# A two-layer graph kernel: its opening reordered, a stream of block products started six instructions earlier, and rows returned in five parts

## The chip, the cores and the metric

The kernel runs on one core of a Trainium2 chip. The metric is the device time of one execution in microseconds (us). A core has five engines with queues of their own: TensorE (PE) for matmuls and transposes, VectorE (DVE), ScalarE (ACT) and GpSimd (POOL) for everything elementwise, and SyncE (SP), which here only issues transfers (DMAs). ACT's queue can issue transfers as well. Each engine runs its instructions in order.

## The reference

x has N = 2708 rows of D = 256; adj is 2708 x 2708, sparse in values but stored dense. Layer 0 makes two steps of a diffusion over adj and of an attention of x with itself that keeps, in each row, only the largest probabilities until their sum reaches 0.9:

```python
R = adj + eye;  R = R / R.sum(-1)
for n in range(2):
    A  = top_p_attention(Xa, W1, W2, W3)     # q = Xa W1' W2', k = Xa W3', softmax, keep the top 0.9, renormalise
    Xf = R @ Xf
    Xa = A @ Xa
    Z += Xf @ U1[n].T + Xa @ U2[n].T
x = layernorm(x + layernorm(x + Z))          # with ln_g, ln_b inside
# layer 1: graph attention, 4 heads of 64
Wh = x @ W;  e_ij = leaky_relu(s_i + s_j);  masked where adj is zero (the diagonal counts as one)
x = layernorm(x + softmax_j(e) @ Wh)
```

## The kernel before

**Tiles.** Rows are cut in 22 tiles: 16 of 128 rows and 6 of 110. Six `groups` hold four tiles each of one height (the last two). All heavy data is float32.

**The opening.** `query_weights` (L736) transposes w1 and multiplies it with w2, so that queries need one product. `turn_x` (L1420) transposes one group of x by TensorE into both halves of one two-bank tile `lg`; ACT copies the first half to `x_turned` (which lies in the buffer `ba`) and DVE the second. `project` (L749) makes keys and queries of a group: the products of both weights go to one bank, DVE copies the key's half (L765, to a buffer that the profile calls junk or kT) and ACT the query's (qT, L766); a DMA brings the copy for the other half of the partitions. A group that crosses a boundary of 512 columns is projected in two halves, both in the same bank.

**Terms and search.** `terms1` (L1253) multiplies a tile of x with U1 of both steps; ACT copies the result (L1263, L1264), and a DMA stores part of it (c1). Between the terms stand `slot`s: each advances generators that are under way. `search` makes a tile's logits (`scores`, L791, exponentials on ACT at L810) and finds the cut of the top 0.9: `candidates` by DVE's Max8 (L913), `settle` by a chain of small DVE instructions and two long passes over the row (L898 and L982, near 3 us each). `layer1_weights` (L1392) loads and prepares weights of layer 1.

**Attention steps.** `step(s, ...)` (L1345) goes over the 22 tiles; `weigh` (L274) multiplies the transposed probabilities of the tile, group by group, with the values. `turned` (L261) does a group's transposes into a bank `tr` (there is one) and an ACT copy to eT (L271); it runs one group ahead of its products. After each group, `between` runs, which calls `slot`. At the end of a tile ACT scales the result (xa, L1363); in step 0 a tile's queries and keys for step 1 follow (`after_attention0`: L774, L761).

**The block products.** R is never multiplied out plainly: POOL (`mixes`, L691) makes sums of quarters of adj, and `walks` (L1051) is a generator in which each `next(stream)` is one matmul of 128 columns (L1130), seven products of 11 matmuls for each pair of tiles in the manner of Winograd. The results are added up on DVE (L1140 y1, L1142 y2, L1148, L1150) and ACT. The operand `xm` and `xe` are re-blended between the two rounds: `reblend` (L1194), on DVE for T3 and T2 (L1024, L1026) in two parts each, the second of which needs the last rows of the first round. In step 1 every slot takes 11 or 12 instructions of the stream.

```python
if last:
    next(stream)              # in `between`, at the last tile of step 0
```

**Layer 1.** Scores of all pairs are formed on DVE (pt, L1644) with masks that come from adj: a DMA (L245, on SP), ACT's sign and square (L247, L248) and DVE's diagonal (L251). TensorE sums values (L1656) and denominators (L1666). It goes over two halves of the rows, g = 0 and 1. `beside(g, i)` (L1737) is called for each column tile i and puts other work between: at (0, 12) the rows kept in DRAM come back (xe<-xd, L1750, in two transfers), at i = 11 a row of sources is shared over the partitions (`share`, L217, and `spread`, L225). The last three tiles of layer 0 get x for their sums from `x_late`, loaded on SP at L1083 behind a POOL memset (L1076).

**Order.** PE, ACT, DVE and POOL run in the order that the program is written in (a manual schedule); SP's transfers are placed by a scheduler. A transfer waits, on its queue, for the landing of the transfer eight before it.

Of the kernel before, what the change touches and what calls it, by code (L numbers as in the profile page):

```python
# [1 line left out]

# [6 lines left out]
F32 = mybir.dt.float32  # L9
# [7 lines left out]
P = 128  # L17
# [3 lines left out]
CHUNK = 512  # L21
# [13 lines left out]


SPEND_BETWEEN, SPEND_1 = 14, (12, 11, 11, 12, 11, 11)
HELD, WAITING = 6, 4
SIDE = 32
LN2 = 0.6931471805599453  # L40
# [5 lines left out]
def kernel(  # L46
# [54 lines left out]

    HALF, PAIRS = D // 2, NT // 2
    xe = const.tile([P, NT, D + 2], F32, name="xe")
    for one in (HALF, D + 1):
        nc.gpsimd.memset(xe[:, :, one : one + 1], 1.0)

    wx = const.tile([P, DC, D + 2 * H], F32, name="wx")
    ident = const.tile([P, P], F32, name="ident")
    make_identity(nc, ident)
    minus_half = const.tile([P, 1], F32, name="minus_half")  # L110
    nc.gpsimd.memset(minus_half, -0.5)

# [7 lines left out]

    LATE = 3
    x_late = const.tile([P, LATE, D], F32, name="x_late")
    engines = {nc.tensor.engine, nc.scalar.engine, nc.vector.engine, nc.gpsimd.engine}

    def load_x(dst):
# [426 lines left out]
    def fast_layer0(ep, adjp):  # L552
# [28 lines left out]
        w1_sb = heldp.tile([P, D], F32, name="xa1")[:DA].rearrange("p (c d) -> p c d", c=DC)  # L581
        nc.scalar.dma_start(w1_raw, w1T.rearrange("(c p) e -> p c e", p=P))
        nc.scalar.dma_start(w2_sb, w2T)
        for h in range(2):
            nc.scalar.dma_start(wkqk[:, :, 2 * h, :], w3T.rearrange("(c p) e -> p c e", p=P))
        xm = keep.tile([P, NT, D], F32, name="xm")
        load_x(xm)
        for s in range(STEPS):
            for k, u in enumerate((u1T, u2T)):
                nc.sync.dma_start(u_sb[:, k, :, s], u[s].rearrange("(c p) e -> p c e", p=P))  # L590
        nc.sync.dma_start(g_sb, ln_g.partition_broadcast(P))
        nc.sync.dma_start(b_sb, ln_b.partition_broadcast(P))
# [143 lines left out]
        def query_weights():  # L736

            tr = free_bank()
            for c in range(DC):
                nc.tensor.transpose(tr[:DA, c, :], w1_raw[:, c, :], ident)  # L740
            nc.vector.tensor_copy(w1_sb, tr[:DA, 0:DC, :])
            for c in range(DC):
                tr = free_bank()
                nc.tensor.matmul(
                    tr[:, 0, :DA], w1_sb[:, c, :], w2_sb, start=True, stop=True
                )
                nc.vector.tensor_copy(wkqk[:, c, 1], tr[:, 0, :DA])

        def project(s, c0, w, pj, xT, copy_q, copy_k):  # L749

            for lo, hi, h in ((c0, min(c0 + w, HN), 0), (max(c0, HN), c0 + w, 1)):
                if lo >= hi:
                    continue
                here, there = slice(h * DA, (h + 1) * DA), slice((1 - h) * DA, (2 - h) * DA)
                at = slice(lo - c0, hi - c0)
                for c in range(DC):  # L760
                    nc.tensor.matmul(  # L761
                        pj[:, at], wkqk[:, c, h : h + 2].rearrange("p h e -> p (h e)"),
                        xT[:, c, at], start=(c == 0), stop=(c == DC - 1),
                    )
                copy_k(kT[s][here, lo - h * HN : hi - h * HN], pj[here, at])  # L765
                copy_q(qT[there, lo:hi], pj[there, at])  # L766
                nc.sync.dma_start(qT[here, lo:hi], qT[there, lo:hi])
# [283 lines left out]
        def walks():  # L1051
# [184 lines left out]
        def after_attention0(t, xa):  # L1236
# [8 lines left out]
            turn(xa, m, tp, nc.scalar.copy, xT)  # L1245
            yield
            if t % 2:
                pj = free_bank().rearrange("p a b -> p (a b)")
                project(1, off[t - 1], 2 * m, pj, both, nc.scalar.copy, nc.scalar.copy)
                yield  # L1250
            terms2(t, xT)

# [89 lines left out]
                if next(stream, True):  # L1342
                    break

        def step(s, cur, spend):  # L1345
            turned_first = None
            for t in range(NT):
                m = rows[t]
                e, rden = ready[t]
# [9 lines left out]
                def between(n):  # L1359
# [11 lines left out]
                    if (s, t) == (0, NT - 1):  # L1371
# [8 lines left out]
                def turn_next(n):  # L1380
                    u = t + n // len(groups)
                    if u == NT:
                        return None
                    return turned(ready[u][0], rows[u], n % len(groups), tpp, ps_tr, nc.scalar.copy)

                turned_first = weigh(
                    ac[:m, :D], turned_first or turn_next(0), m,
                    lambda j: cur[: rows[j], j, 0:D], turn_next, between,
                )
                ready.pop(t)  # L1390

        def layer1_weights():  # L1392
# [2 lines left out]
            wg = tmp[:, 0 : DC * D].rearrange("p (c h o) -> p c h o", c=DC, h=H)  # L1395
            ga = tmp[:, DC * D : DC * D + 2 * D].rearrange("p (h o) -> p h o", h=H)
            pr = tmp[:, DC * D + 2 * D : DC * D + 3 * D].rearrange("p (h o) -> p h o", h=H)
            for c in range(DC):
                nc.sync.dma_start(
                    wg[:, c], gat_w[:, c * P : (c + 1) * P, :].rearrange("h p o -> p h o")  # L1400
                )
            nc.sync.dma_start(
                ga.rearrange("p h o -> p (h o)"),
                gat_a.rearrange("h o u -> (h o u)").partition_broadcast(P),
            )
            for c in range(DC):
                nc.gpsimd.tensor_copy(wx[:, c, 0:D], wg[:, c].rearrange("p h o -> p (h o)"))
                for k in range(2):
# [11 lines left out]
        def turn_x(grp):  # L1420
            k = rows[grp[0]]
            w, c0 = k * len(grp), off[grp[0]]
            tp = ps_lg.tile([P, 2, CHUNK], F32, name="lg")
            for c in range(DC):
                for q, t in enumerate(grp):
                    nc.tensor.transpose(
                        tp[:, c, q * k : (q + 1) * k], xm[:k, t, c * P : (c + 1) * P],
                        ident[:k, :k],
                    )
            for c, copy in enumerate((nc.scalar.copy, nc.vector.tensor_copy)):  # L1430
                copy(x_turned[:, c, c0 : c0 + w], tp[:, c, :w])
            return c0, w

        with tc.manual_schedule(engines=engines):
            query_weights()
            ahead = turn_x(groups[0])
            for n in range(len(groups)):
                c0, w = ahead
                if n + 1 < len(groups):
                    ahead = turn_x(groups[n + 1])  # L1440
                pj = free_bank().rearrange("p a b -> p (a b)")
                project(
                    0, c0, w, pj, x_turned[:, :, c0 : c0 + w],
                    nc.scalar.copy, nc.vector.tensor_copy,
                )
            ahead = []
            for n in range(10):
# [3 lines left out]
            layer1_weights()  # L1451
            begun.append(True)
            step(0, xm, [0] * len(groups))
# [9 lines left out]
            step(1, ba, SPEND_1)  # L1463
            owed[0] = 0
            while doing:
                slot(NT)
# [67 lines left out]
    def layer1(ep, adjp, r=None, verdict=None, early=()):  # L1534
# [197 lines left out]
        if verdict:  # L1732
            late += [[2 * k, prepared(NT - LATE + k)] for k in range(LATE)]
            late.append([NT + 4, verdict(aux)])
        rest, running = [], []

        def beside(g, i):  # L1737

# [5 lines left out]
            for part in list(running):  # L1744
                if next(part, running) is running:
                    running.remove(part)
            if fast and (g, i) == (0, 12):
                nc.gpsimd.memset(xe[:, 0 : NT - LATE, 0:1], 0.0)
                for t0, t1 in ((0, 16), (16, NT - LATE)):
                    nc.sync.dma_start(  # L1750
                        xe[: rows[t0], t0:t1, 0:D], xd[: rows[t0], t0:t1, :]
                    )
# [116 lines left out]
```

## Time and profile before

| | before |
|---|---|
| median of 3 runs | 1526.68 us (1526.19 to 1529.36) |
| profiled execution | 1526.18 us |
| its span in the trace | 1524.3 us |
| PE busy | 1484.9 us, 97% |
| DVE busy | 1282.0 us, 84% |
| ACT busy | 810.0 us, 53% |
| POOL busy | 594.4 us, 39% |
| moved by DMA | 255.98 MB |
| mean granted clock of TensorE | 0.996 |

The profile's page gives busy time by engine and then the span in 40 slices, in tenths. A timeline lists an engine's instructions in order of time, neighbours of one kind put together: start, length, engine, line, operation, output and inputs with shapes, and in brackets the idle time just before and the instruction that ended it. SPq and ACTq are the issues of transfers.

### The profile page before, as it was taken

To read this page: it belongs to the slowest core of one execution; us is meant where nothing else is said; L and a number is where in the kernel's file an instruction comes from. 1 tells how busy PE (TensorE), PEld (TensorE's weight loads), DVE (VectorE), ACT (ScalarE), POOL (GpSimd) and SP (SyncE) were. 2 spreads that over 40 slices of the span, in tenths; PEclk is the share of its full clock that TensorE was granted. 3 is DMA by queue.
4 is the path that set the end of the run, shared out by engine and by line. 5 is a ranking of instruction groups with operands and counts; after the bars stand their busy time and mean duration, and the time that the engine had idled before them with its cause. 6 is when DMAs were issued, how large, how long until landed. Compare 5 with 4: busy or idle time off the path is not lost. (4 is left out here: it accounts for less than half of the span.)

```text
span 1524.3 us, 30055 instructions
## 1 busy us (share of the span) xinstructions
PE 1484.9 (97%) x10537; PEld 1072.8 (70%) x10537; DVE 1282.0 (84%) x3749; ACT 810.0 (53%) x1535; POOL 594.4 (39%) x979
## 2 busy tenths in 40 slices
PE   8999999999999999999999999999999999999996
PEld 4377777777778889988988888888898423333343
DVE  3689999998515978888889898999896998999996
ACT  3444454445326556655655666666653444456474
POOL 0057675763013223223454554544553210045143
PEclk9999999999999999999999999999999999999998
DMA  6568988885037645554564555555464455334331
GB/s 166 149 208 280 280 278 260 256 239 184 10 116 245 202 153 171 167 154 144 159 193 143 163 187 170 185 167 178 132 177 158 117 174 167 98 108 132 89 106 53
DMA packets 214489, 255.98 MB, mean 168 GB/s; under 512 B 42145, under 2 KB 180541, under 8 KB 214329
## 3 DMA queue, kind: packets, MB, share of 16 engines
q1 hardware_dynamic: 205622, 246.62, 54.0%
q10 hardware_dynamic: 8707, 7.35, 1.6%
q8 instruction: 85, 1.39, 0.4%
q14 instruction: 75, 0.61, 0.1%
HBM read 190.10 MB, written 62.44 MB: 166 GB/s over the span
## 5 line engine op out<-in xcount | busy, mean ns | idle before, releaser
L271 ACT COPY eT<-tr 128x512 f32<-128x512 f32 (+5 forms) x264 | 141.6, 536 | 239.5 <-PE tr L266 236.7
L833 ACT ACTIVATE junk<-e,minus,rth 128x2708 bf16<-128x2708 f32 (+1 forms) x88 | 232.8, 2646 | 52.4 <-POOL rth L865 51.7
L284 PE MATMUL att<-ba,eT 128*128 128x256 f32 (+3 forms) x968 | 231.5, 380 | 0.0
L284 PE MATMUL att<-xm,eT 128*128 128x256 f32 (+3 forms) x968 | 230.8, 379 | 0.3 <-ACT xa L1363 0.3
L1656 PE MATMUL acc<-pt,v 128*32 128x512 f32 (+3 forms) x2112 | 218.2, 543 | 1.0
L1644 DVE SCALAR_TENSOR_TENSOR pt<-e,tj,blk 128x1024 f32<-128x1024 f32 (+3 forms) x176 | 185.0, 1115 | 6.7 <-DMA blk<-in_adjT_dram 3.6
L284 PEld LDWEIGHTS att<-ba,eT 128*128 128x128 f32 (+3 forms) x968 | 170.0, 187 | 22.2 <-ACT eT L271 0.8
L284 PEld LDWEIGHTS att<-xm,eT 128*128 128x128 f32 (+3 forms) x968 | 169.5, 186 | 22.0 <-ACT xa L1363 0.7
L1130 PE MATMUL walk<-xe,blk 128*128 128x128 f32 (+3 forms) x1386 | 173.1, 275 | 0.9 <-ACT xw L1144 0.4
L1130 PEld LDWEIGHTS walk<-xe,blk 128*128 128x128 f32 (+1 forms) x1386 | 164.4, 187 | 12.6 <-issue 8.2
L1656 PEld LDWEIGHTS acc<-pt,v 128*32 128x32 f32 (+1 forms) x2112 | 75.7, 109 | 124.2 <-issue 75.9
L266 PE MATMUL tr<-ident,e 128*128 128x128 f32 (+3 forms) x968 | 146.9, 270 | 5.1 <-ACT eT L271 5.1
L810 ACT ACTIVATE e<-lg 128x1024 f32<-128x1024 f32 (+3 forms) x112 | 106.7, 957 | 63.3 <-PE lg L791 63.1
L266 PEld LDWEIGHTS tr<-ident,e 128*128 128x128 f32 (+3 forms) x968 | 113.3, 139 | 34.9 <-issue 12.2
L1130 PE MATMUL walk<-xm,blk 128*128 128x128 f32 (+3 forms) x1034 | 130.7, 276 | 6.1 <-DVE u_sb L1140 3.3
L1130 PEld LDWEIGHTS walk<-xm,blk 128*128 128x128 f32 (+3 forms) x1034 | 123.4, 187 | 15.4 <-issue 6.9
L1666 PE MATMUL acc<-pt,sb 128*32 128x512 f32 (+3 forms) x1056 | 113.6, 542 | 0.0
L913 DVE MAX8 cand<-e 128x8 f32<-128x170 f32 (+1 forms) x352 | 86.4, 320 | 29.6 <-ACT e L810 20.0
L1644 DVE SCALAR_TENSOR_TENSOR pt<-r,tj,blk 128x1024 f32<-128x1024 f32 (+1 forms) x88 | 110.0, 1313 | 1.1 <-issue 0.3
L247 ACT ACTIVATE blk<-blk 128x1024 f32<-128x1024 f32 (+3 forms) x66 | 63.3, 961 | 80.2 <-DMA blk<-in_adjT_dram 68.9
L913 DVE MAX8 cand<-scr 128x8 f32<-128x97 f32 (+1 forms) x616 | 102.8, 244 | 0.0
L817 POOL TENSOR_TENSOR fact<-zp 128x1 f32<-128x1 f32 (+1 forms) x44 | 41.0, 932 | 157.4 <-ACT e L810 157.4
(288 smaller groups left out, 2480.5 us busy)
## 6 DMA issues: line engine op xcount, KB each, us to landing
blk<-in_adjT_dram SPq DMA_DIRECT2D x68, 512.0 KB
blk<-S SPq DMA_DIRECT2D x48, 512.0 KB
blk<-D SPq DMA_DIRECT2D x24, 512.0 KB
blk<-in_adjT_dram SPq DMA_DIRECT2D x26, 440.0 KB
D<-blk SPq DMA_DIRECT2D x16, 512.0 KB
S<-scr SPq DMA_DIRECT2D x16, 512.0 KB
S<-blk SPq DMA_DIRECT2D x16, 512.0 KB
xm<-S SPq DMA_DIRECT2D x16, 512.0 KB
```

Source lines behind the costliest of these rows:

```text
L247: nc.scalar.activation(bar, bar, AF.Sign)
L266: nc.tensor.transpose(tr[: rows[t], q, :m], e[:m, off[t] : off[t + 1]], ident[:m, :m])
L271: copy(eT[:k, : len(grp), :m], tr[:k, : len(grp), :m])
L284: nc.tensor.matmul(acc, eT[: rows[t], q, :m], value(t), start=(t == 0), stop=(t == NT - 1),)
L810: nc.scalar.activation(halves[:m, :, c0 : c0 + w], lg[:m, :, :w], AF.Exp, accum_out=zp[:m, n : n + 1],)
L817: nc.gpsimd.tensor_add(z, zp[:m, 0:1], zp[:m, 1:2])
L833: nc.scalar.activation(junk[:m], e[:m], func, scale=rth, bias=minus1[:m], accum_out=acc)
L913: nc.vector.max(cand[:, n, :], src[:m, n * size : min(N, (n + 1) * size)])
L1130: nc.tensor.matmul(ac, blk[:k, j, :], MOVING[name](j, k, w), start=start and j == 0, stop=j == PAIRS - 1, skip_group_check=True,)
L1644: nc.vector.scalar_tensor_tensor(pt[:k, :gw], targets[g][h // 2][:k, h % 2, :gw], tj[:k, j, h : h + 1], bar, op0=ALU.max, op1=ALU.mult,)
L1656: nc.tensor.matmul(acc[h // 2][c][to : to + SIDE, :w], v[j][:k, h, o : o + SIDE], probs[n][h][:k, c0 : c0 + w], **at,)
L1666: nc.tensor.matmul(acc[2][c][h * SIDE : (h + 1) * SIDE, :w], sb[:k, j, h : h + 1].to_broadcast([k, SIDE]), probs[n][h][:k, c0 : c0 + w], **at,
```

## The change

- The opening: POOL makes the identity first. `wake` puts a DVE memset and five matmuls on it at the start of TensorE's program. Group 0 of x is transposed ahead of w1, and w1·w2 follows group 1's transposes. `turn_x` takes two separate banks (att and tr, or two lg) in turn, and each half of a projection takes a bank of its own. w3 is loaded once, and POOL makes its second copy.
- Loads: u2T, the layer-1 weights, ln_g and ln_b go from SP's queue to ACT's, between the first `terms1`. `x_late`'s memset is at the very start, for all three tiles at once; the scheduler then puts its loads behind those of u1T on SP.
- The first transposes and eT copy of a step are made earlier: for step 0 ahead of the last two `terms1`, for step 1 ahead of the last slot before it.
- At the last tile of step 0, seven calls of `next(stream)` (one for loads, six matmuls) in place of one.
- `reblend` gives way once after its first parts; in DVE's order y1's add (L1140 before) then stands ahead of the tile's settling.
- The rows come back in five transfers, called at i = 4, 6, 8, 10 and 12. In SP's order they stand together: three behind the ninth mask load of layer 1, two behind the tenth.

```diff
+HEAD = 7
...
+    make_identity(nc, ident)              # ahead of the other memsets
...
+    nc.gpsimd.memset(x_late[:, :, 0:1], 0.0)
...
-        for h in range(2):
-            nc.scalar.dma_start(wkqk[:, :, 2 * h, :], w3T.rearrange("(c p) e -> p c e", p=P))
+        nc.scalar.dma_start(wkqk[:, :, 0, :], w3T.rearrange("(c p) e -> p c e", p=P))
...
+        load_u(0, u1T, nc.sync)
...
             nc.vector.tensor_copy(w1_sb, tr[:DA, 0:DC, :])
+            yield
+            nc.gpsimd.tensor_copy(wkqk[:, :, 2, :], wkqk[:, :, 0, :])
...
+                pj = free_bank().rearrange("p a b -> p (a b)")    # in project, per half
...
-                    nc.gpsimd.memset(ca[:, 0:1], 0.0)
...
             for name in ("T3", "T2"):
                 blend(name, *J_PARTS[0])
+            yield
             while owing:
                 yield
...
-                            next(stream)
+                            for _ in range(HEAD):
+                                next(stream)
...
+            load_u(1, u2T, nc.scalar)     # in layer1_weights, with yields between,
+            yield                         # and gat_w, gat_a, ln_g, ln_b likewise
...
-            tp = ps_lg.tile([P, 2, CHUNK], F32, name="lg")
+            if groups.index(grp) % 2:
+                homes = [ps_lg.tile([P, 2, CHUNK], F32, name="lg")[:, 0] for _ in range(DC)]
+            else:
+                homes = [
+                    ps_at.tile([P, CHUNK], F32, name="att"),
+                    ps_tr.tile([P, 4, P], F32, name="tr").rearrange("p a b -> p (a b)"),
+                ]
...
+        def wake():
+            idle = ps_lg.tile([P, 2, CHUNK], F32, name="lg")
+            some = ba.rearrange("p t d -> p (t d)")[:, :D]
+            nc.vector.memset(some, 1.0)
+            for _ in range(5):
+                nc.tensor.matmul(idle[:, 0, :D], some[:, :P], some, start=True, stop=True)
...
-            query_weights()
+            wake()
             ahead = turn_x(groups[0])
+            weighing = query_weights()
+            next(weighing)
...
                 if n + 1 < len(groups):
                     ahead = turn_x(groups[n + 1])
+                next(weighing, None)
...
+                if n in (1, 2, 3):
+                    next(more)
                 for t in range(n * NT // 10, (n + 1) * NT // 10):
+                    if t == NT - 2:
+                        eT = turn_next(0, 0)
                     terms1(t, x_turned[:, :, off[t] : off[t + 1]])
...
+                    if (t, n) == (2, 2):
+                        eT = turn_next(0, 0)
...
+        BACK = {4: (0, 4), 6: (4, 8), 8: (8, 12), 10: (12, 16), 12: (16, NT - LATE)}
...
-            if fast and (g, i) == (0, 12):
-                nc.gpsimd.memset(xe[:, 0 : NT - LATE, 0:1], 0.0)
-                for t0, t1 in ((0, 16), (16, NT - LATE)):
+            if fast and g == 0 and i in BACK:
```

More of the change, by code (lines that the diff above doesn't have):

```diff
@@ L1 @@
 from contextlib import ExitStack
+from functools import partial
 import concourse.bass as bass
@@ L103 @@
     xe = const.tile([P, NT, D + 2], F32, name="xe")
+    ident = const.tile([P, P], F32, name="ident")
+    make_identity(nc, ident)
     for one in (HALF, D + 1):
@@ L107 @@
     wx = const.tile([P, DC, D + 2 * H], F32, name="wx")
-    ident = const.tile([P, P], F32, name="ident")
-    make_identity(nc, ident)
     minus_half = const.tile([P, 1], F32, name="minus_half")
@@ L583, in fast_layer0, with load_u @@
         nc.scalar.dma_start(w2_sb, w2T)
-        for h in range(2):
-            nc.scalar.dma_start(wkqk[:, :, 2 * h, :], w3T.rearrange("(c p) e -> p c e", p=P))
+        nc.scalar.dma_start(wkqk[:, :, 0, :], w3T.rearrange("(c p) e -> p c e", p=P))
         xm = keep.tile([P, NT, D], F32, name="xm")
         load_x(xm)
[L588 to L592, printed above, removed]
+        def load_u(k, u, queue):
+            for s in range(STEPS):
+                queue.dma_start(u_sb[:, k, :, s], u[s].rearrange("(c p) e -> p c e", p=P))
+        load_u(0, u1T, nc.sync)
         def constant(name, value, width=1, pool=w0):
@@ L747, in query_weights, with project @@
                 nc.vector.tensor_copy(wkqk[:, c, 1], tr[:, 0, :DA])
-        def project(s, c0, w, pj, xT, copy_q, copy_k):
+        def project(s, c0, w, xT, copy_q, copy_k):
             for lo, hi, h in ((c0, min(c0 + w, HN), 0), (max(c0, HN), c0 + w, 1)):
@@ L1247, in after_attention0 @@
             if t % 2:
-                pj = free_bank().rearrange("p a b -> p (a b)")
-                project(1, off[t - 1], 2 * m, pj, both, nc.scalar.copy, nc.scalar.copy)
+                project(1, off[t - 1], 2 * m, both, nc.scalar.copy, nc.scalar.copy)
                 yield
@@ L1343, in slot, with turn_next, step @@
                     break
-        def step(s, cur, spend):
-            turned_first = None
+        def turn_next(t, n):
+            u = t + n // len(groups)
+            if u == NT:
+                return None
+            return turned(ready[u][0], rows[u], n % len(groups), tpp, ps_tr, nc.scalar.copy)
+        def step(s, cur, spend, eT=None):
             for t in range(NT):
@@ L1376, in between @@
                         if last:
-                            next(stream)
+                            for _ in range(HEAD):
+                                next(stream)
                     slot(spend[n], (s, t + 3) if n == len(groups) - 1 - s else None)
[L1380 to L1388, printed above, removed]
+                eT = weigh(
+                    ac[:m, :D], eT or turn_next(t, 0), m,
+                    lambda j: cur[: rows[j], j, 0:D], partial(turn_next, t), between,
                 )
@@ L1397, in layer1_weights @@
             pr = tmp[:, DC * D + 2 * D : DC * D + 3 * D].rearrange("p (h o) -> p h o", h=H)
+            load_u(1, u2T, nc.scalar)
+            yield
             for c in range(DC):
-                nc.sync.dma_start(
+                nc.scalar.dma_start(
                     wg[:, c], gat_w[:, c * P : (c + 1) * P, :].rearrange("h p o -> p h o")
                 )
-            nc.sync.dma_start(
+            nc.scalar.dma_start(
                 ga.rearrange("p h o -> p (h o)"),
@@ L1405, in layer1_weights @@
             )
+            yield
+            nc.scalar.dma_start(g_sb, ln_g.partition_broadcast(P))
+            nc.scalar.dma_start(b_sb, ln_b.partition_broadcast(P))
+            yield
             for c in range(DC):
@@ L1422, in turn_x @@
             w, c0 = k * len(grp), off[grp[0]]
-            tp = ps_lg.tile([P, 2, CHUNK], F32, name="lg")
-            for c in range(DC):
+            if groups.index(grp) % 2:
[5 more added lines that the diff above has]
+                ]
+            for c, home in enumerate(homes):
                 for q, t in enumerate(grp):
                     nc.tensor.transpose(
-                        tp[:, c, q * k : (q + 1) * k], xm[:k, t, c * P : (c + 1) * P],
+                        home[:, q * k : (q + 1) * k], xm[:k, t, c * P : (c + 1) * P],
                         ident[:k, :k],
@@ L1430, in turn_x @@
             for c, copy in enumerate((nc.scalar.copy, nc.vector.tensor_copy)):
-                copy(x_turned[:, c, c0 : c0 + w], tp[:, c, :w])
+                copy(x_turned[:, c, c0 : c0 + w], homes[c][:, :w])
             return c0, w
+        def wake():
[4 more added lines that the diff above has]
+                nc.tensor.matmul(idle[:, 0, :D], some[:, :P], some, start=True, stop=True)
         with tc.manual_schedule(engines=engines):
-            query_weights()
+            wake()
             ahead = turn_x(groups[0])
+            weighing = query_weights()
+            next(weighing)
             for n in range(len(groups)):
@@ L1440, in fast_layer0 @@
                     ahead = turn_x(groups[n + 1])
-                pj = free_bank().rearrange("p a b -> p (a b)")
+                next(weighing, None)
                 project(
-                    0, c0, w, pj, x_turned[:, :, c0 : c0 + w],
+                    0, c0, w, x_turned[:, :, c0 : c0 + w],
                     nc.scalar.copy, nc.vector.tensor_copy,
@@ L1446, in fast_layer0 @@
             ahead = []
+            more = layer1_weights()
             for n in range(10):
                 slot(0, (0, n // 4) if n in (0, 4, 9) else None)
+                if n in (1, 2, 3):
+                    next(more)
                 for t in range(n * NT // 10, (n + 1) * NT // 10):
+                    if t == NT - 2:
+                        eT = turn_next(0, 0)
                     terms1(t, x_turned[:, :, off[t] : off[t + 1]])
-            layer1_weights()
+            list(more)
             begun.append(True)
-            step(0, xm, [0] * len(groups))
+            step(0, xm, [0] * len(groups), eT)
             while doing:
@@ L1462, in fast_layer0 @@
                         break
-            step(1, ba, SPEND_1)
+            step(1, ba, SPEND_1, eT)
             owed[0] = 0
@@ L1746, in beside @@
                     running.remove(part)
-            if fast and (g, i) == (0, 12):
-                nc.gpsimd.memset(xe[:, 0 : NT - LATE, 0:1], 0.0)
-                for t0, t1 in ((0, 16), (16, NT - LATE)):
-                    nc.sync.dma_start(
-                        xe[: rows[t0], t0:t1, 0:D], xd[: rows[t0], t0:t1, :]
-                    )
+            if fast and g == 0 and i in BACK:
+                t0, t1 = BACK[i]
+                if t0 == 0:
+                    nc.gpsimd.memset(xe[:, 0 : NT - LATE, 0:1], 0.0)
+                nc.sync.dma_start(xe[: rows[t0], t0:t1, 0:D], xd[: rows[t0], t0:t1, :])
             if rest and i >= 2 and i % 2 == 0:
```

## Prediction

> **What bounds the kernel.** First the page's busy shares, then its slices, then TensorE's waits with the timeline around each of the longest.
>
> ```profile
> span 1524.3 us, 30055 instructions
> ...
> PE 1484.9 (97%) x10537; PEld 1072.8 (70%) x10537; DVE 1282.0 (84%) x3749; ACT 810.0 (53%) x1535; POOL 594.4 (39%) x979
> ...
> PE   8999999999999999999999999999999999999996
> ...
> PEclk9999999999999999999999999999999999999998
> ```
>
> TensorE is busy 97% of the span, and in no slice but the first and last under nine tenths. What can be won is therefore idle time of TensorE and time at a low clock, nothing else; what DVE (84%), ACT and POOL do costs only where TensorE waits for it. Charging every matmul what it costs in a stretch without waits (a 512-column record 429 ns, a 256-column one 216, a walk's 128-column one 112, a transpose 109), I count 1417 us of work; the other 107 us are lost. Most is spread at 0.5 to 1 us per 20 us; the lumps are the first 80 us (17), the end (12), 400 to 520 (14), 780 to 820 (7), 1160 to 1180 (2.3) and 1220 to 1280 (6). Timelines of TensorE there (start, length, engine, line, what, count; in brackets the idle time ahead and its releaser):
>
> ```profile
> 5.05 0.61 PE L740 MATMUL walk<-ident,xa 128*64 128x128 f32 x2 [5.05 <-DMA xa<-in_w1T_dram]
> ...
> 7.62 3.67 PE L1426 MATMUL lg<-ident,xm 128*128 128x128 f32 x16
> 11.09 2.98 PE L761 MATMUL walk<-ba,wkqk 128*128 128x512 f32 x4
> ...
> 14.78 1.88 PE L761 MATMUL walk<-ba,wkqk 128*128 128x512 f32 x4
> ...
> 20.25 0.88 PE L761 MATMUL walk<-ba,wkqk 128*128 128x182 f32 x4 [1.60 <-ACT qT L766]
> ...
> 26.25 1.99 PE L791 MATMUL lg<-junk,qT 64*128 64x512 f32 x8
> ```
> ```profile
> 75.16 0.66 PE L266 MATMUL tr<-ident,e 128*128 128x128 f32 x4 [0.83 <-ACT eT L271]
> ...
> 437.06 0.41 PE L774 MATMUL lg<-ident,xa 110*128 110x110 f32 x2 [0.56 <-ACT xa L1363]
> ...
> 510.01 0.66 PE L266 MATMUL tr<-ident,e 128*128 128x128 f32 x4 [0.68 <-ACT eT L271]
> ...
> 797.39 2.50 PE L1130 MATMUL walk<-xm,blk 128*128 128x128 f32 x14 [2.94 <-DVE u_sb L1140]
> ...
> 1177.90 0.59 PE L266 MATMUL tr<-ident,e 110*110 110x110 f32 x4 [1.81 <-ACT eT L271]
> ...
> 1271.52 1.14 PE L171 MATMUL aux<-wx,xT 128*110 128x264 f32 x4 [1.29 <-ACT xT L167]
> ```
>
> In the first fence the 16 transposes take 3.67 us where 8 take 1.04 after 13.9, and the first projection 2.98 where the next takes 1.88: TensorE runs at half rate until about 13.3. The second fence has the waits that the change touches. Who is late is seen on the other engines:
>
> ```profile
> 785.29 2.70 DVE L1024 TENSOR_TENSOR xm<-xe 110x384 f32<-110x384 f32 x1 [2.73 <-POOL xe L1231]
> ...
> 797.05 0.29 DVE L1140 TENSOR_TENSOR u_sb<-walk,u_sb 128x128 f32<-128x128 f32 x1
> ...
> 1162.46 0.30 SPq L1083 DMA_DIRECT2D x_late<-in_x_dram  x1
> ...
> 1174.89 1.06 ACT L247 ACTIVATE blk<-blk 128x1024 f32<-128x1024 f32 x1 [1.85 <-DMA blk<-in_adjT_dram]
> ...
> 1241.12 0.38 SPq L1750 DMA_DIRECT2D xe<-xd  x1
> ...
> 1255.42 5.81 SPq L225 DMA_DIRECT2D r<-shared  x4
> 1261.32 5.13 SPq L245 DMA_DIRECT2D blk<-in_adjT_dram  x3
> ...
> 1271.27 0.29 DVE L251 TENSOR_TENSOR blk<-blk,ident 128x128 f32<-128x128 f32 x1 [5.21 <-ACT blk L248]
> ```
>
> **The opening.** Before, TensorE waits for w1 (5.0), for w2 (6.6), and only then transposes x, although x's first group had landed at 4.85. After: five 128x256 matmuls on a memset tile from about 1.1 us (ten records of 0.427 at half rate, to 5.4), then group 0, w1's two, group 1 (landed 6.4), w1·w2, projection 0. The five need none of the inputs and end at about the time the first can start, so they cost at most 0.5 us; POOL's ident is done at 2.1 already. The last input of projection 0 is wkqk: w2 lands at 6.0, w3 at 7.8, POOL's copy of w3 is 0.3 or so, DVE's two copies are 0.22 each behind a product at 7.7 to 8.0. So projection 0 starts at about 8.9 against 11.09. From there to the first logits (26.25) TensorE has 11.98 us of full-rate work and spends 15.16: 1.1 half rate in projection 0, 1.60 where the second half of projection 2 waits for ACT's copy out of the same bank (the row at 20.25), 0.5 small. The change gives the half its own bank and lets ACT and DVE copy two banks of transposes at once (six times DVE's copy waited on ACT's). If the clock is up: 8.9 + 12.0 + 0.4 = 21.3, gain 4.9. If half rate lasts to 12: about 24, gain 2.3.
>
> Here the trace and a rule differ. The trace: without a break from 6.6, full rate only at 13.3, 6.7 us later, of which real matmuls were 1.0 and then, from 11.09, 2.2; and after the stall at 794 half rate lasted from 798.3 to 801.7, 3.4 us of uninterrupted work. The Trainium skill ("TensorE: Matmul & The Clock Gate", Part 1) puts the switch after about 3.4 us of sustained activity in a window that runs freely from the kernel's start. By the rule the five matmuls (4.3 us) have TensorE warm between 4.5 and 8: gain 4.9. By the 6.7 us of this trace it would be warm at 7.8 at the earliest, with the transposes counted; if only matmuls count and the pauses at 6 to 8 reset it, at 12: gain 2.3. I take 4.4, ends 2 and 5.5.
>
> **Moved loads.** SP loses u2T, gat_w, gat_a, ln_g, ln_b (seven issues of 0.34 to 0.47); ACT gets them between terms1 of tiles 2 to 8. ACT needs 0.75 us of copies per terms1 while TensorE needs 1.72, so 0.45 fits; and u2T is not needed before step 0's end. DMA i waits for DMA i-8 to land, so a late landing would hold ACT, and with it the copies TensorE waits for; landings at that time take 2 to 3 us and none is queued. Cost 0, ends 0 and +1.5. On SP the last x load no longer stands behind w1's landing (it was issued at 4.93, landed 13.1). x_late's three loads (0.33 MB) come to SP's start: 2 us of traffic before the mask blocks are asked for, 0.
>
> **First transposes.** At 74.06 and 508.7 TensorE makes a row's first transposes and then waits for ACT's copy (1.00 and 0.84 us lost between starts). With that copy two terms1 (3.4 us) or a slot earlier, both go: -1.0 and -0.8. Their input is ready (final passes end at 45.0 and 500.9), so nothing new is waited for.
>
> **Head start of the stream.** At 436.1 the last row of step 0 waits 0.73 us for ACT's scaling. Six walk matmuls (6 x 0.111 = 0.67), of blocks long landed, now fill it: -0.65. They were due anyway. But the stream then runs six places ahead in all of step 1, and the adds of the walks on DVE (L1140, L1142, L1148, L1150) stand up to 14 places earlier in DVE's order. What waits on these today: 1.47 us at 490, 1.66 at 504.6, 0.50 at 516.9, about 1.1 each at 901, 1033 and 1095. They may vanish or come elsewhere: 0, ends -3 and +3.
>
> **Reblend.** At 794.3 TensorE wants product 7 and waits 3.11 us for y1's add (the row at 797.05), which stands on DVE behind reblend part 1 (held by POOL to 785.29, done at 788.6), 14 maxima to 790.9 and 6.2 us of settling. The changed order has reblend part 0, maxima, part 1, maxima, y1, then settling: y1 is done at 791.2, before it is wanted. Off: 3.1 for the wait, and 1.7 for the 3.4 us at half rate behind it (8 transposes and products of 798.3 to 801.7), together 4.8. Late next would be the add of the following product behind DVE's pass of 3.04 us at 809; the order puts it at 812 again, while TensorE, 5 us earlier, wants that bank at about 814. I take 4.5, ends 3 and 5.
>
> **SP ahead of layer 1.** SP stood from 1152.2 to 1162.46 on x_late's load, which waited for POOL's memset behind POOL's long queue. Behind it on SP: the first mask, issued 1165.2, landed 1174.8; ACT waited 1.85 us for it (row 1174.89), with the eT copy queued behind, and TensorE 1.97 between starts. The memset is now at the start, so the mask is asked for up to 10 us sooner: -1.9, ends -2.5 and -1.
>
> **Rows back.** xe<-xd (2.1 MB, from 1241.1, landing near 1250) is ahead of the share at 1249.85, which lands at 1255.3; the spread's four 512 KB follow at 1255.4 and the mask behind them at 1261.32. DVE idles 1.27 and 5.21 us (row 1271.27), TensorE 1.29. In SP's new order the return's parts stand five mask loads earlier, three (1.5 MB) after the ninth and two (0.8) after the tenth, about 1209 to 1215. The share then lands some 3.4 us sooner, DVE's idle time falls to 3, and TensorE's goes: -1.4. Against it 1.5 MB at 200 GB/s is 7.5 us in front of one mask load; those lead their use by about 8. Ends -3 and +2.
>
> **Sum.** 4.4 + 1.0 + 0.65 + 0.8 + 4.5 + 1.9 + 1.4 = 14.65. The profiled execution took 1526.18 (span 1524.3 and 1.9 around it), 0.5 under the median 1526.68: 1526.2 - 14.65 = 1511.5, against the median 1512.0. As each stall removed leaves a small one, I give back 0.5: 1512.5. A measurement of this kernel can tell about 0.2%, 3 us.
>
> **Rivals.**
> (a) The opening stays cold and the reblend's stall moves on to the next product: gains 2 there, 2 here, and the rest 5.75 minus a mask load's 1.5: 8.3, so 1518. For it: the 6.7 us at half rate; DVE is at 92% from 790 to 810. Against: ten records without a break stand ahead now. Chance 0.24.
> (b) Slower: the six-place shift sets the walks' adds behind DVE's passes of 3.03 and 3.04 us (two per row) once in each of step 1's 22 rows. Today such a wait costs 1.5 (490, 504.6), so it could cost 1.5 x 22 = 33: 1512 + 33 = 1545; it decides from 14.65 / 22 = 0.67 us per row, and 1530 is reached at 0.82. For it: three such waits within 30 us at 490 to 517. Against: between 520 and 780 nearly none, the adds have a whole product (4.6 us) before their bank is wanted, and the new order leaves them as near behind the passes as before. Chance 0.11, and 0.05 for a shift that only eats the gain (1524 to 1529).
> (c) The same shift clears 490, 504.6, 517 and half of the later ones: 4 us more, 1508. Chance 0.15.
> (d) The sum as it stands, 1509 to 1515: 0.45.
>
> Faster by over 0.2%: (a) + (c) + (d) = 0.84; within: 0.05; slower: 0.11. The range from 1505 (c with its ends) to 1522 ((a) with its costs) leaves out (b) and a little at the bottom.
>
> **What would show it.** Right: projections at 0.43 us per record from the first, logits near 21; no idle bracket at the first transposes of either step; product 7 without a wait and slices 780 to 820 at full clock; no SP gap of 10 us near 1155; DVE's idle at 1265 halved. Wrong: transposes of 213 ns after 8 us; new waits of TensorE on L1140 to L1150 (their new line numbers) once per row; mask loads late near 1215.

## The result and the profile after

| | before | after |
|---|---|---|
| median of 6 runs | 1527.18 us (1525.58 to 1529.36) | 1516.53 us (1515.10 to 1517.71) |
| profiled execution | 1526.18 us | 1516.33 us |
| its span | 1524.3 us | 1514.5 us |
| PE, DVE busy | 1484.9, 1282.0 us | 1485.1, 1282.9 us |

The ratio after to before is 0.9929, with a 95% interval of 0.9917 to 0.9942: 10.65 us faster by the medians, 9.85 by the profiled executions. The prediction's point was 1512.5, a gain of some 14; about 4 us of it did not arrive. The page of after, the lines that answer to those shown of before:

```profile
span 1514.5 us, 30074 instructions
...
PE 1485.1 (98%) x10547; PEld 1068.2 (71%) x10547; DVE 1282.9 (85%) x3750; ACT 808.8 (53%) x1535; POOL 596.7 (39%) x978
...
PE   9999999999999999999999999999989999999996
...
PEclk9999999999999999999999999999999999999998
```

TensorE's busy time is what it was, though the five new matmuls are in it; the span lost nearly 10 us of idle time. The slices show no more than that the first one is full now, and that the 30th is not. To see where time came from, I take landmarks that both traces have (the first matmul of a kind, or of a row, which is one of a step's 22 tiles) and set their times against each other:

| landmark | before, us | after is ahead by, us | change on the way |
|---|---|---|---|
| first logits | 26.25 | 4.90 | +4.90 |
| first product of step 0 | 75.66 | 5.65 | +0.75 |
| last product of step 0 | 436.12 | 6.38 | +0.73 |
| first product of step 1 | 510.50 | 4.29 | -2.09 |
| row 9 of step 1 | 782.20 | 4.87 | +0.58 |
| row 10 | 817.22 | 9.66 | +4.79 |
| row 19 | 1109.50 | 9.40 | -0.26 |
| row 20 | 1137.05 | 3.21 | -6.19 |
| layer 1, one eighth in | 1226.95 | 7.48 | +4.27 |
| last matmul | 1511.42 | 9.53 | +2.05 |

Two steps go the wrong way: 2.1 us between the attention steps, and 6.2 between rows 19 and 20. (At the entry of layer 1 TensorE's order differs between the two kernels, so I take no landmark there.) TensorE's timeline of after, first the opening and the places of the prediction's other steps:

```profile
1.17 4.63 PE L1458 MATMUL lg<-ba 128*128 128x256 f32 x10 [1.17 <-DVE ba L1456]
5.60 0.71 PE L1444 MATMUL att<-ident,xm 128*128 128x128 f32 x4
...
9.13 1.96 PE L768 MATMUL walk<-ba,wkqk 128*128 128x512 f32 x4 [0.37 <-issue]
...
21.35 1.99 PE L798 MATMUL lg<-junk,qT 64*128 64x512 f32 x8
...
70.00 1.89 PE L287 MATMUL att<-xm,eT 128*128 128x256 f32 x8
...
431.29 0.35 PE L781 MATMUL lg<-ident,xa 110*128 110x110 f32 x2
...
500.03 0.71 PE L1136 MATMUL walk<-xm,blk 128*128 128x128 f32 x4 [1.74 <-DVE xw L1156]
...
501.26 3.56 PE L1136 MATMUL walk<-xm,blk 128*128 128x128 f32 x18
...
786.43 0.60 PE L269 MATMUL tr<-ident,e 128*128 128x128 f32 x4
...
788.60 2.17 PE L1136 MATMUL walk<-xm,blk 128*128 128x128 f32 x18
...
1120.05 0.40 PE L269 MATMUL tr<-ident,e 110*110 110x110 f32 x2 [0.79 <-ACT eT L274]
...
1125.20 0.57 PE L269 MATMUL tr<-ident,e 110*128 110x110 f32 x4 [0.62 <-DVE e L989]
...
1132.54 0.77 PE L1136 MATMUL walk<-xe,xm 128*110 128x128 f32 x2 [3.52 <-DVE xw L1154]
```

The transposes are at 109 ns from 5.8 us on, projection 0 runs at 9.13, the logits at 21.35. At 431.29, 786 and 70.0 the brackets of before are gone. But 500.03 has a wait of 1.74 us, and from 500.7 on half rate follows (18 matmuls take 3.56 us at 501.26, where 18 take 2.17 at 788.60), and at 1120 to 1132 there are three waits that before did not have: 0.79, 0.62 and 3.52 us. DVE's timeline of after tells the last ones:

```profile
1105.61 0.29 DVE L1146 TENSOR_TENSOR u_sb<-walk,u_sb 110x128 f32<-110x128 f32 x1 [4.12 <-PE walk L1136]
...
1122.02 3.03 DVE L989 SCALAR_TENSOR_TENSOR e<-scr,fact,e 110x2708 f32<-110x2708 f32 x1
...
1128.10 3.47 DVE L905 SCALAR_TENSOR_TENSOR scr<-e,hi 110x2708 f32<-110x2708 f32 x1
...
1132.21 0.28 DVE L1154 TENSOR_TENSOR xw<-walk,u_sb 110x128 f32<-110x128 f32 x1
```

The same settling in before starts without a wait, and y1's add comes in its midst, without a wait too:

```profile
1111.52 0.19 DVE L926 TENSOR_REDUCE fact<-cand 110x1 f32<-110x28 f32 x1
...
1119.49 0.29 DVE L1140 TENSOR_TENSOR u_sb<-walk,u_sb 110x128 f32<-110x128 f32 x1
```

In after DVE stands 4.12 us for the product of TensorE that y1's add (L1146, before L1140) takes, at 1105.61; that add is now right ahead of a tile's settling, so all of the settling starts late. Its passes end at 1125.0 and 1131.5. TensorE waits for the first (row 1125.20), and for an add (L1154, row 1132.21) that stands behind the second. The wait of 0.79, for ACT's copy, I have not followed back.

### The profile page after: what moved, and what is told of

It is laid out like the page before. It is cut to its first block, busy times and chain, and to the rows that moved or that the text cites. A ratio compares the mean times of both kernels' runs of the same rounds, so it can differ in the third digit from the quotient of the medians.

```text
span 1514.5 us, 30074 instructions
## 1 busy us (share of the span) xinstructions
PE 1485.1 (98%) x10547; PEld 1068.2 (71%) x10547; DVE 1282.9 (85%) x3750; ACT 808.8 (53%) x1535; POOL 596.7 (39%) x978
## 5 line engine op out<-in xcount | busy, mean ns | idle before, releaser
L1691 PEld LDWEIGHTS acc<-pt,v 128*32 128x32 f32 (+1 forms) x2112 | 71.4, 110 | 126.6 <-issue 91.5
```

The costliest lines, as they stand in the source:

```text
L1691: nc.tensor.matmul(acc[h // 2][c][to : to + SIDE, :w], v[j][:k, h, o : o + SIDE], probs[n][h][:k, c0 : c0 + w], **at,)
```

## The experiments

The figures below are medians in us, with the lead over before at the last matmul of the profiled execution behind them where it says more. Single runs of one kernel differ by up to 12 us here, and mostly the slower had the lower mean clock of TensorE (one kernel: 1512.3 at 0.997, 1524.4 at 0.991), so the stages of a trace are read first.

### Fewer matmuls ahead

```diff
-HEAD = 7
+HEAD = 4
```

> Four calls of the stream at the end of step 0 (three matmuls ahead) instead of seven (six ahead); all else as after. Theory A, the six-place head start makes the new stall: with six ahead, y1's add of the last pair but one stands in DVE's order in front of a tile's settling, DVE idles 4.12 us for it at 1105.6, and TensorE then waits 0.79, 0.62 and 3.52 us at 1120 to 1132 and loses about 1.7 at half clock. With three ahead the add stands behind the settling again: no such idle time, no wait over 1.2 us near 1130, 5 to 6 us less in the stretch of rows 19 to 20, time 1511. Theory B, the stall comes from TensorE having won 5 us at the reblend while DVE won nothing, so that DVE is the bound late in step 1: the wait stays within 1 us, time 1516.5.

Measured: 1510.16, ratio to before 0.9896 (0.9882 to 0.9911), lead 15.55. It has the lowest median of all kernels here, and its interval lies wholly under that of after. DVE and then TensorE of this kernel at the same place:

```profile
1099.47 0.19 DVE L933 TENSOR_REDUCE fact<-cand 110x1 f32<-110x28 f32 x1
...
1107.84 0.29 DVE L1146 TENSOR_TENSOR u_sb<-walk,u_sb 110x128 f32<-110x128 f32 x1
...
1125.21 0.08 DVE L905 DVE_READ_ACCUMULATOR scr<-e,hi 110x1 f32 x1
...
1129.09 0.27 DVE L1154 TENSOR_TENSOR xw<-walk,u_sb 110x128 f32<-110x128 f32 x1
```
```profile
1117.11 0.35 PE L269 MATMUL tr<-ident,e 110*110 110x110 f32 x2
...
1121.43 0.54 PE L269 MATMUL tr<-ident,e 110*128 110x110 f32 x4
...
1129.40 2.44 PE L1136 MATMUL walk<-xe,xm 128*110 128x128 f32 x20 [0.35 <-DVE xw L1154]
```

Settling starts at 1099.47 with no bracket, and y1's add follows in the midst of it at 1107.84 without a wait; the second pass ends at 1125.3 rather than 1131.5. Of three waits, 0.35 us is left. Rows 19 to 20: nothing lost (lead 11.40 at both). Between the steps it gains 1.0 where after lost 2.1.

```diff
-HEAD = 7
+HEAD = 1
```

> One call of the stream at the end of step 0, as before the change; all else as after. Theory A: the stall near 1130 is gone, the wait of 0.73 us at the end of step 0 is back, time 1511.5. Theory B: the stall stays, time 1517.

Measured: 1511.56, lead 14.81; no stall near 1130 (lead 11.26 at rows 19 and 20), and the wait at the end of step 0 is back (0.73 between starts). Theory A holds twice, B falls: with the new re-blending and without the six places, the stall is not there.

### The old order of the re-blending

```diff
                 blend(name, *J_PARTS[0])
-            yield
             while owing:
```

> The re-blending without the extra yield, so that y1's add stands behind the settling again; all else as after. Both theories: the wait for product 7 (3.1 us) and the half clock behind it (1.7) are back near 786. Theory A: the stall near 1130 stays, time 1516.5 + 4.8 = 1521. Theory B: TensorE is 4.8 us later there and the stall near 1130 is gone or under 1 us, time 1516 to 1517.

Measured: 1518.07, lead 8.53. The stall near 1130 stays (rows 19 to 20 lose 5.6): B falls again. But the expectation for product 7 was wrong. TensorE loses 1.68 us between starts there, with no half clock, and not to y1's add. DVE, ACT and TensorE of this kernel:

```profile
781.83 0.28 DVE L1146 TENSOR_TENSOR u_sb<-walk,u_sb 128x128 f32<-128x128 f32 x1
782.02 0.20 DVE L933 TENSOR_REDUCE fact<-cand 128x1 f32<-128x28 f32 x1
```
```profile
782.53 0.39 ACT L857 ACTIVATE rth<-slope,nguess,y 128x1 f32<-128x1 f32 x1 [6.24 <-POOL slope L853]
782.95 2.64 ACT L840 ACTIVATE junk<-e,minus,rth 128x2708 bf16<-128x2708 f32 x1
...
785.59 0.56 ACT L274 COPY eT<-tr 128x512 f32<-128x512 f32 x1
```
```profile
786.21 0.66 PE L269 MATMUL tr<-ident,e 128*128 128x128 f32 x4 [1.52 <-ACT eT L274]
```

With the stream six places ahead, y1's add (781.83) stands ahead of the settling (782.02) even in the old order, so the wait for it is gone whole. The 1.68 is another wait: transposes for ACT's copy to eT, which stands behind a pass of 2.64 us that ACT could only start when POOL, which finished its own part of the re-blending at 781.1, had made slope. So I ran both undone:

```diff
-HEAD = 7
+HEAD = 1
...
-            yield                  # in reblend
```

> One call of the stream and the old re-blending: the change without these two parts. If the two take the same wait away, each alone gains it and together they gain it once: here product 7's wait of 3.1 us and the half clock behind it are whole, 4.8 over the run with one call, 1516.3. If the old re-blending costs only the 1.7 that it cost with seven calls: 1513.2.

Measured: 1518.45, lead 9.63. TensorE's timeline:

```profile
786.88 1.05 PE L1136 MATMUL walk<-xe,blk 128*128 128x128 f32 x8
790.89 2.46 PE L1136 MATMUL walk<-xm,blk 128*128 128x128 f32 x14 [2.96 <-DVE u_sb L1146]
793.14 1.06 PE L269 MATMUL tr<-ident,e 128*110 128x128 f32 x4
```

The wait for y1's add is whole (2.96 in the bracket, 3.13 between starts), and the transposes at 793.14 take 1.06 us where four take 0.60 at full rate. From row 9 to row 10 this kernel gains 0.0 and the one with one call 4.7. So each of the two parts takes the wait for y1's add by itself, and the clock's loss with it; the head start without the new order leaves the other wait of 1.7 in its place, so the re-blending beside it is worth 1.7 (gains of 4.79 and 3.14 from row 9 to 10), and alone 4.7.

### The head start alone

```diff
                         if last:
-                            next(stream)
+                            for _ in range(7):
+                                next(stream)
```

> The kernel before, with seven calls of the stream at the end of step 0 and nothing else changed. Theory A: the wait of 0.73 at 436 is filled, some 1.5 to 3 us are lost at 480 to 510, the wait of 3.11 us for product 7 shrinks to about 1.7, as it does where the old re-blending stands with seven calls, with or without the half clock behind it, and the stall near 1130 appears (5 to 6 us): in all slower than before by 2 to 6, 1529 to 1533. Theory B (the stall needs the gain of the new re-blending): no stall near 1130, 1524 to 1526.

Measured: 1526.27, ratio to before 0.9998 (0.9990 to 1.0007): nothing. The trace shows why the expected loss is not there: rows 9 to 10 gain 3.1 (product 7's wait and the clock's loss go, the wait of 1.7 for ACT's copy comes), rows 19 to 20 lose 6.2, the rest comes back by layer 1. The same idle time stands on DVE's timeline of this kernel, and the same wait on TensorE's:

```profile
1112.12 0.29 DVE L1140 TENSOR_TENSOR u_sb<-walk,u_sb 110x128 f32<-110x128 f32 x1 [4.12 <-PE walk L1130]
```
```profile
1139.09 0.76 PE L1130 MATMUL walk<-xe,xm 128*110 128x128 f32 x2 [3.54 <-DVE xw L1148]
```

This is the old kernel with one number changed, so the stall is the head start's and needs nothing else of the change. The shift that puts y1's add ahead of the settling gains at row 9, where the product is ready, and loses at row 19, where it is not.

### The lead given back in row 16

```diff
-                    slot(spend[n], ...)
+                    slot(spend[n] - (s and t == 16), ...)
```

> As after (seven calls at the end of step 0), but in tile 16 of step 1 each of the six slots takes one instruction of the stream less, so that from tile 17 on the stream stands where one call would have put it. The work is the same. Theory A (where y1's add stands in DVE's order near tile 19 makes the stall): the waits of 480 to 505 and the half clock behind them stay as in after, DVE's idle time of 4 us at 1105 and TensorE's of 3.5 at 1129 go, gain over after 5 to 6, time 1511. Theory B' (what counts is only that the stream has won time early, in 480 to 510): the stall stays, 1516.5.

Measured: 1516.31 (1514.01 to 1518.48), lead 12.22 in the profiled execution against 9.53 of after. DVE's idle time at 1105 and TensorE's stall are gone (lead 8.69 at row 19 and 8.68 at row 20), so where the stream stands at row 19 makes the stall. The gain is half of what was expected, though, 2.7 in the traces and none that the medians show: the stall's 6.2 us are partly given back later. From row 19 to the end this kernel's lead grows by 3.53 and that of the kernel with one call by 3.55, after's by 0.13: there the stall costs 3.4 us in the end, 1.7 of it half clock behind the wait. (The 0.7 between 3.4 and 2.7 is the six matmuls, done in the rows after 16.) In the run with x_late's old memset below, whose clock held there, that lead grows by 1.56, so the stall costs 2.0. What after loses between the steps stays here: from the end of step 0 to row 9 the lead shrinks by 1.51 in after, by 1.59 here and by 0.07 with one call. But these two are the only ones of six traces with the seven calls in the new kernel that ran at half clock there (0.83 from 500 to 510); in the other four the lead grows by 0.04 to 0.45. The trace with one call ran at half clock too, from 480 to 490. So that loss goes with the clock of an execution and is not shown to be the six places' own. By the medians the kernel with one call is 5.0 faster than after, and the one with the lead given back 0.2; how the 5.0 divides between the stall and the rest stays open.

### The opening without its five matmuls

```diff
-            wake()
             ahead = turn_x(groups[0])
```

> Without the five matmuls on a memset tile (and without the memset); all else as after. If the five matmuls bring the clock up: group 0's transposes at 213 ns, first logits at 23 to 24.5 instead of 21.35, 2 to 3 us slower (1519). If the new order of the opening is all that counts: logits at 21.3 to 21.8, no measurable difference.

Measured: 1518.43 (1514.38 to 1521.76). In the profiled execution the first transposes take 213 ns and the logits start at 22.45, 1.1 later, which is less than expected. Another 5.1 us are lost in step 0 at one place, near 335: TensorE waits 3.25 for a pass of DVE and runs at half clock behind it (0.83 from 340 to 350). DVE came there 7.5 us later than in after, because it had stood twice for POOL:

```profile
288.45 0.28 DVE L943 SCALAR_TENSOR_TENSOR sums<-sums,tau,top 128x56 f32<-128x56 f32 x1 [3.08 <-POOL tau L829]
...
307.20 1.12 DVE L943 SCALAR_TENSOR_TENSOR sums<-sums,tau,top 128x56 f32<-128x56 f32 x1 [3.85 <-POOL tau L829]
```

POOL itself had waited 8.34 us for a block of adj, to 270.55 (5.86 in after, to 263.90). Why that block was late stays open, and I could not tie it to the opening. I asked again on the quieter base of four calls:

> Four calls, without the five matmuls at the start. From the run with seven calls and without them: half rate to about 8.9 us, first logits 1.1 later, 1511.3. If they do more than that (a clock that slips more often later): 1513 or more.

Measured: 1511.63, 1.5 more than with them, though the intervals of the two overlap; the logits start at 24.53, 2.9 later. TensorE's timeline:

```profile
5.41 1.09 PE L1444 MATMUL att<-ident,xm 128*128 128x128 f32 x4 [5.41 <-DMA xm<-in_x_dram]
...
10.46 3.77 PE L768 MATMUL walk<-ba,wkqk 128*128 128x512 f32 x4
14.03 0.68 PE L1444 MATMUL att<-ident,xm 128*128 128x128 f32 x4
```

The projection at 10.46 takes 3.77 us, half rate throughout, though TensorE had worked since 5.41; in the other run without the five it ran at full rate, in 1.95 from 10.23. So without them the clock came up at 8.9 in one run and at 14 in the other; with them it was up by 6 in the traces of both after and the kernel with four calls.

### The rows back in two transfers

```diff
-            if fast and g == 0 and i in BACK:
+            if fast and (g, i) == (0, 12):       # two transfers, as before
```

> The rows back in two transfers at i = 12 of g = 0, as before the change; all else as after. If the five parts are worth what the prediction says: DVE idle over 6 us and TensorE 1.3 to 2 near 1255 to 1265, 1.4 to 2 us slower, 1518. If the wait belongs to the share's and spread's own transfers: no difference (within 0.4), 1516.5.

Measured: 1520.71 (1517.5 to 1522.15). In the profiled execution the lead grows only from 8.05 to 8.60 between the first and third eighth of layer 1, where after goes from 7.48 to 9.52: 1.5 us. DVE's idle time there, two parts first and then five:

```profile
1262.66 0.29 DVE L254 TENSOR_TENSOR blk<-blk,ident 128x128 f32<-128x128 f32 x1 [4.75 <-ACT blk L251]
```
```profile
1261.75 0.29 DVE L254 TENSOR_TENSOR blk<-blk,ident 128x128 f32<-128x128 f32 x1 [3.29 <-ACT blk L251]
```

It is 4.75 (over 6 was expected) and 3.29 us, in both beside the same 1.27; TensorE waits 0.84 in the one (1.32 between starts) and not in the other. The median's 4 us more are not explained by this place.

### x_late's memset back in its place

```diff
-    nc.gpsimd.memset(x_late[:, :, 0:1], 0.0)
...
+                    nc.gpsimd.memset(ca[:, 0:1], 0.0)    # in the walks, as before
```

> x_late's memset back where it was, in front of each of its three loads in step 1; all else as after. If the memset behind POOL's queue holds SP: a pause of SP of 5 to 10 us near 1145, the first mask late, TensorE waits near 1166, 1 to 2 us slower, 1518. If the stall at 1129 has given SP the time anyway: no difference.

Measured: 1516.98 (1512.34 to 1524.41), lead 13.40: nothing lost to after; of the 3.9 by which the lead is larger, 3.4 are that this run kept full rate behind the waits near 500 and 1130. SP's pause ahead of x_late's loads is 4.3 us there, and the mask is not late for TensorE. Whether the stall at row 20 covers the pause is asked with four calls, where there is no stall:

> Four calls of the stream (no stall near 1130), with x_late's memset back in front of its three loads in step 1. If the memset behind POOL's queue is what held the first mask: SP stands 5 to 10 us near 1140, ACT waits for the first mask, TensorE waits 1 to 2 us ahead of layer 1 near 1160, 1512. If in the run with seven calls it cost nothing because it costs nothing: within 0.5 of 1510.2.

Measured: 1516.83 where 1512 was expected, 6.7 more than with the memset at the start; 4.2 by the traces (leads of 11.33 and 15.55), of which 1.7 are half clock (0.83 from 1170 to 1180). SP's, ACT's and TensorE's timelines of it:

```profile
1139.76 0.76 SPq L692 DMA_DIRECT2D blk<-D  x2
1151.10 0.30 SPq L1089 DMA_DIRECT2D x_late<-in_x_dram  x1
```
```profile
1158.18 1.06 ACT L249 ACTIVATE blk<-blk 128x1024 f32<-128x1024 f32 x1 [2.57 <-DMA blk<-in_adjT_dram]
...
1167.53 1.06 ACT L249 ACTIVATE blk<-blk 128x1024 f32<-128x1024 f32 x1 [3.54 <-DMA blk<-in_adjT_dram]
```
```profile
1170.75 1.67 PE L1691 MATMUL acc<-pt,v 128*32 128x512 f32 x12 [4.22 <-ACT cs L183]
```

SP issues nothing from 1140.5 to 1151.1; the masks are late twice (2.57 and 3.54 us of ACT), and TensorE waits 4.22 us at the entry of layer 1 for ACT's work behind them.

### The first transposes back in their place

```diff
-                    if t == NT - 2:
-                        eT = turn_next(0, 0)
...
-                    if (t, n) == (2, 2):
-                        eT = turn_next(0, 0)
```

> Four calls, with the first transposes of both steps back where they were. If both waits for the first eT copy come back whole: 1.0 and 0.84 us, 1512.0. If the waits for adds at 480 to 505 take step 1's part over: about 1.0 in all, 1511.2.

Measured: 1513.31 against 1510.16, lead 13.27 against 15.55: 2.3 us. TensorE's timeline at the two places:

```profile
70.68 0.66 PE L269 MATMUL tr<-ident,e 128*128 128x128 f32 x4 [1.39 <-ACT eT L274]
...
505.10 0.66 PE L269 MATMUL tr<-ident,e 128*128 128x128 f32 x4 [0.68 <-ACT eT L274]
```

Step 0's wait is 1.55 between starts (1.0 was expected), step 1's 0.84. They add to the other waits; nothing takes them over.

## Why the prediction was right, and where it was not

By its steps:

- **The opening**, 4.4 predicted, 4.90 measured. The clock was up at 5.8 us, inside the 4.5 to 8 that I had estimated from the rule of the Trainium skill ("TensorE: Matmul & The Clock Gate", Part 1), and not at the 7.8 or 12 that the trace of before would have had it. The rule was the better guide here; the 6.7 us at half rate before were one draw. The runs without the five matmuls show other draws: 3.5 us (5.44 to 8.9) and 8.6 (5.41 to 14.0). The second is longer than two of that page's windows of 3.4 us, so the rule as I used it does not hold for every run. Rival (a)'s cold opening did not happen.
- **First transposes**, 1.8 predicted; 2.3 where they were undone.
- **Re-blending**, 4.5 predicted, 4.79 from row 9 to 10, and 4.7 where it alone differs with one call. Beside six places it is worth 1.7, since the head start, which I gave no part in this wait, takes it too. The place that I named as late next did not wait.
- **SP ahead of layer 1**, 1.9 predicted. In the kernel with one call, whose stream stands as in before, the wait is gone and the lead grows by 1.9 from row 20 to layer 1's first product. Undone, the term depends on its neighbour: nothing where the stall at row 20 stands; 4.2 with four calls, 1.7 of it half clock.
- **Rows back**, 1.4 predicted, 1.5 by the traces. DVE's idle time in front of the diagonal was to fall to 3; it fell to 3.29. The mask loads near 1215 cost nothing.
- **Moved loads**, 0 predicted; no run undid them; the stage of the terms lost 0.3 us in after and nothing in the kernel with four calls. (The load of x that the prediction has at 4.93 is the fifth; the last was issued at 5.34, and at 5.12 in after.)
- **Head start of the stream**, 0.65 of gain predicted, with "0, ends -3 and +3" for its adds. This is the step that failed. The wait of 0.73 was filled as said, but by the medians the kernel with one call is 5.0 faster than after. What the traces show of it is the stall at row 20: 3.4 us in the end in after, 1.7 of that half clock, and 2.0 in a run whose clock held. The rest of the 5.0 stays open: after's profiled execution lost 1.4 more than one call between the steps, but at half clock, which four of six traces with seven calls did not have there, and the run that takes the stall alone away is not faster by its medians. Of the waits that the step listed as waits for the adds, the three at 901, 1033 and 1095 were ended by copies of ACT (eT, cs, eT), not by adds on DVE.

Without that step the sum was 14.0; the kernel with one call gained 14.8 by its trace, and 15.65 by the medians of its session. So rival (b) had the mechanism in part, adds of the walks behind DVE's passes, and its price was wrong: not 0.67 or more in each of 22 rows but once in row 20, 6.2 us of which 2.8 came back. The measured 1516.5 lies nearest to rival (a)'s 1518, and neither of (a)'s reasons came true: that is chance. What I had looked at was where the adds stand against the two long passes, and that is nearly as before. What decided was one add in front of a tile's settling rather than behind it: there the engine that waits is DVE, for TensorE, and TensorE's own waits come 14 to 27 us later.

The clock behind new waits was not in the sum: after's profiled execution runs at half rate behind the waits at 500 and 1132 (granted clock 0.83 in the ten microseconds around each). The kernel with four calls has none there:

```profile
core 0: us, PE busy (x) PEld busy (x) DVE busy (x) ACT busy (x) POOL busy (x), PEclk, DMA share, GB/s
...
500.00:510.00 10.00, 9.97 (x67) 9.76 (x68) 9.42 (x47) 6.98 (x8) 4.77 (x11) 0.83 0.57 175
...
1130.00:1140.00 10.00, 7.46 (x43) 6.58 (x44) 9.72 (x45) 2.89 (x12) 0.54 (x1) 0.83 0.61 175
```
```profile
500.00:510.00 10.00, 9.39 (x69) 8.79 (x68) 9.48 (x49) 7.18 (x9) 4.65 (x13) 1.00 0.76 240
...
1130.00:1140.00 10.00, 10.00 (x75) 9.15 (x74) 9.41 (x39) 2.98 (x12) 2.13 (x3) 1.00 0.48 149
```

PEclk is the third column from the right: 0.83 twice against 1.00 twice. 17% of 10 us is 1.7 us each, in these executions; the section on the lead given back has those where the clock held.

## What to carry to other kernels

When an engine's queue is in program order, moving one engine's work ahead moves every dependent instruction of the others in their order; look for the dependent that lands in front of a long private chain, because the engine then idles for its producer, and the bill comes one chain later. Two edits that take the same wait away gain it once, and an edit behind a stall gains nothing until the stall is gone: price edits together, or undo them on a base without the stall. A head start is a phase, not a quantity: three places were worth 6 us more than six.

## What the runs showed of the hardware

- In the two runs without the five matmuls, TensorE worked from 5.44 and 5.41 us with pauses under 0.4 us, and half rate lasted 3.5 us in one and 8.6 in the other, over the same instructions. In the first, full rate came after nothing but transposes. With five matmuls of 256 columns from 1.17 us on, full rate was there at 5.8 in after and at 5.9 in the kernel with four calls.
- In after a wait of 1.9 us between starts at 498 was followed by half rate for some 3.4 us (granted clock 0.83 from 500 to 510), and one of 3.7 at 1129 likewise (0.83 from 1130 to 1140); in the run with x_late's old memset place, waits of 1.93 and 3.70 at the same instructions were followed by full rate (1.00 twice). The length of a wait does not settle whether the clock falls.
- In after and in the run of seven calls without the five matmuls, one DVE instruction over 56 columns took 7.27 and 7.33 us and the next one 2.95 in both (over 48 columns, in the timelines of row 19, the two take 0.27 and 0.21). POOL ran elementwise instructions of about 1.1 us beside them without a pause, and each of the four ended within 0.1 us of the end of one of POOL's. So DVE can be held over more than one instruction of POOL. In after TensorE did not wait for it. What held DVE stays open.
